# Five score runs for two groups of heads instead of six, with the values' products in the same step, and another rule for the order of the queues

## The chip, the cores and the metric

The kernel runs on one core of a Trainium2 chip. Its engines are named as in the profile: PE (TensorE) multiplies matrices, DVE (VectorE), ACT (ScalarE) and POOL (GpSimd) work on elements, and SP (SyncE) issues most of the DMA transfers. The metric is the device time of one execution in microseconds (us), as the median of several runs.

## The reference

The program is one transformer layer in which attention and a ternary feed-forward network read the same normalized input, and both are added to the input. There are 16 batch rows of 512 tokens, width 512, 16 heads of 32, hidden width 1408. Attention is causal.

```python
def layer(x, w_qkv, b_qkv, w_out, b_out, gate_w, up_w, down_w, gate_s, up_s, down_s):
    xn = layernorm(x)                                     # over 512
    q, k, v = split_heads(xn @ w_qkv.T + b_qkv)           # 16 heads of 32
    scores = q @ k.T / sqrt(32)
    attn = softmax(where(causal, scores, -inf))
    a = merge_heads(attn @ v) @ w_out.T + b_out
    g = (xn @ gate_w.T) * gate_s                          # weights in {-1, 0, 1}
    u = (xn @ up_w.T) * up_s
    f = ((silu(g) * u) @ down_w.T) * down_s
    return x + a + f
```

## The kernel before

**Precision by halves.** Every float32 operand of a product is split into two 16-bit parts, high and low. A product of two split operands is three matmuls (high-high, high-low, low-high), and one with a ternary weight, which is exact in eight bits, is two. So the queries and keys of a group of heads are 12 matmuls of 512 columns each, one hidden chunk of 128 (`ffn_chunk`) is 8 for the gate and 8 for the up projection, a down tile of 128 tokens is 22 and an output tile is 12. All of these go through `mm_group` (line 260) and use the whole 128 x 128 array. The low part comes from a subtraction, on GpSimd for queries and keys (479), hidden values (737) and attention outputs (701), and on VectorE for values (507) and probabilities (621).

**Groups, slots and runs.** Four heads are a group, as they fill the 128 partitions. There are 16 x 4 = 64 groups, and each has a slot of the program. The scores of a group (`soft_run`) are made by blocks of 128 queries: block i sees (i + 1) x 128 keys. Scores of four heads go through four 32-row parts of the array at once (`tile_position`), into four PSUM buffers "s1", one for each head. A group has three runs: block 3 (512 columns), block 2 (384), and blocks 1 and 0 (256 + 128). All three want the same four buffers. For each block and head VectorE takes the row maximum (591), and ScalarE the exponential with its sum (596). Then a block's probabilities of all heads are split into two 16-bit parts (ScalarE 616, VectorE 621) in a buffer "pq", and a DMA transpose that SP issues (630) writes them, transposed, to `pT`, which has one copy. Before, "pq" has two buffers of 4096 elements, and each block is one piece: 2048, 1536, 1024 and 512 elements.

**Values.** `av_step` multiplies `pT` with the values: 72 matmuls on 32-column parts of the array (686). They wait for all four transposes of the group, and the next group's transposes wait for them. `R` is the transposed reciprocal of the exponential sums.

**Fillers.** `fillers` gives each slot full-array work: the queries and keys of the next slot, and the batch row's values, hidden chunks, down tiles and, one row later, output tiles. They use three PSUM buffers "mm".

**The order.** Nothing runs in the order of the program text. Every piece is a `Step` with an engine, an expected duration, a latency and what it reads and writes. `Plan.order` lays all steps out in time by these expected figures: for PE by a key, which spreads fillers and runs over the slot, and at most 20 us ahead of the earliest key that is still open (`AHEAD`); for the other engines by the time a step became ready plus a fixed slack. The steps are then issued in that order, and on the chip each engine keeps it. `begin` asks whether a buffer of a ring is free.

**The start.** The first x, the weights for queries, keys and values and small constants are loaded by SP; gate, up and down weights, which are converted on the way, by nine transfers of GpSimd (`load_gu`, `load_wd`, lines 305 and 314), all after the first queries and keys ("first"). The output weights come in slot 2 (`load_wo`). The residual of a down tile loads x again and adds it and the bias (764 to 768).

## Time and profile before

| | us |
|---|---|
| median of three runs (lowest, highest) | 1895.2 (1893.14, 1897.84) |
| the profiled execution's own time | 1895.28 |
| its span, first to last instruction | 1893.5 |
| PE busy | 1856.3 |
| VectorE busy | 1526.5 |
| ScalarE busy | 1377.2 |
| GpSimd busy | 846.2 |

In the lines shown below, each engine has its busy time, its share of the span and its number of instructions. A line of a timeline gives start, length, engine, line of the kernel, operation, output and inputs, shape and count, and in brackets how long the engine was idle before and what ended that. Matmuls are pipelined: the length of one is longer than the distance from its start to the next. A line of the waits gives who waited for whom, the total, how often, and the longest. A line of a group of instructions ends with busy time, mean length in ns, and idle time before. In a table by stretches, the last three numbers are the granted TensorE clock, the share of the DMA engines that is busy, and GB/s.

### The profile page before, as it was taken

The numbers are of one execution on the slowest core, as the hardware profiler recorded it, in microseconds if no ns is written. First come the engines' busy times: TensorE is split into PE (matmuls) and PEld (weight loads), VectorE is DVE, ScalarE is ACT, GpSimd is POOL, SyncE is SP. The second block draws the span as 40 slices with busy tenths as digits, with TensorE's granted clock in tenths as the row PEclk, the third lists the DMA queues.
The fourth block names the chain that finished last, engine by engine and source line by source line (L and its number), as shares of the span: only waits on it lengthen the run. The fifth ranks groups of instructions, "written<-read, shape, count | busy, mean of one in ns | idle before, by whom it ended". The sixth has DMA issues, their size and how long they took to land. (4 is left out here: it accounts for less than half of the span.)

```text
span 1893.5 us, 40528 instructions
## 1 busy us (share of the span) xinstructions
PE 1856.3 (98%) x15006; PEld 863.7 (46%) x15006; DVE 1526.5 (81%) x3665; ACT 1377.2 (73%) x3179; POOL 846.2 (45%) x649
## 2 busy tenths in 40 slices
PE   7889999999999999999999999999999999999998
PEld 3344444444444444444444444444444444444443
DVE  7888779787887978969788687887979779687684
ACT  6777767778677777777768686786766867777773
POOL 3364444444454444443444444444444444344552
PEclk9999999999999999999999999999999999999999
DMA  8875777777777768767767777587686777676755
GB/s 167 148 160 116 137 148 144 135 143 138 154 143 154 144 129 156 141 145 145 134 136 159 147 152 128 133 157 145 142 148 137 135 162 142 140 144 125 134 112 119
DMA packets 838030, 268.89 MB, mean 142 GB/s; under 512 B 801985, under 2 KB 808513, under 8 KB 837825
## 3 DMA queue, kind: packets, MB, share of 16 engines
q1 hardware_dynamic: 833200, 264.07, 71.4%
q0 software_dynamic: 4624, 2.16, 1.4%
q8 instruction: 119, 1.95, 0.4%
q14 instruction: 87, 0.70, 0.1%
HBM read 55.59 MB, written 16.78 MB: 38 GB/s over the span
## 5 line engine op out<-in xcount | busy, mean ns | idle before, releaser
L596 ACT ACTIVATE p<-s,negm 128x512 f32<-128x512 f32 (+3 forms) x1024 | 531.1, 534 | 267.0 <-DVE negm L591 262.8
L621 DVE SCALAR_TENSOR_TENSOR pq<-p,pq 128x2048 f16<-128x2048 f32 (+3 forms) x256 | 413.8, 1623 | 150.1 <-ACT pq L616 149.2
L591 DVE CUSTOM_DVE_ANT_0 s<-s,mask 128x512 f32<-128x512 f32 (+3 forms) x1024 | 473.1, 518 | 38.5 <-PE s L562 25.3
L737 POOL TENSOR_TENSOR hl<-ft,hh 128x512 f16<-128x512 f32 x176 | 246.1, 1400 | 372.8 <-ACT hh L736 372.6
L616 ACT ACTIVATE pq<-p 128x2048 f16<-128x2048 f32 (+3 forms) x256 | 325.8, 1287 | 8.7 <-DMA pT<-pq 7.3
L260 PE MATMUL u<-xh,wu 128*128 128x512 f16 x704 | 267.4, 380 | 9.4 <-DVE ft L727 6.4
L479 POOL TENSOR_TENSOR qkl<-qkt,qkh 128x512 f16<-128x512 f32 x128 | 160.0, 1250 | 248.0 <-ACT qkh L477 247.6
L260 PE MATMUL g<-xh,wg 128*128 128x512 f16 x704 | 268.0, 381 | 0.3 <-DVE ft L727 0.3
L260 PE MATMUL g<-xl,wg 128*128 128x512 f16 x704 | 267.3, 380 | 0.0
L260 PE MATMUL dn<-wd,hh 128*128 128x512 fp8e4 x704 | 267.3, 380 | 0.0
L260 PE MATMUL u<-xl,wu 128*128 128x512 f16 x704 | 267.3, 380 | 0.0
L260 PE MATMUL dn<-wd,hl 128*128 128x512 fp8e4 x704 | 266.8, 379 | 0.0
L596 ACT ACTIVATION_READ_ACCUMULATOR p<-s,negm 128x1 f32 x1024 | 217.2, 212 | 0.0
L260 PEld LDWEIGHTS <-wu 128*128 128x128 fp8e4 x1408 | 136.4, 98 | 176.8 <-issue 15.1
L260 PEld LDWEIGHTS <-wg 128*128 128x128 fp8e4 x1408 | 134.0, 98 | 164.5 <-issue 7.7
L701 POOL TENSOR_TENSOR ol<-Rs,oh 128x512 f16<-128x512 f32 x64 | 103.3, 1613 | 203.0 <-ACT oh L700 202.8
L736 ACT CAST hh<-ft 128x512 f16<-128x512 f32 x176 | 110.1, 626 | 97.3 <-DVE ft L733 96.6
L727 DVE SCALAR_TENSOR_TENSOR ft<-ft,g 128x512 f32<-128x512 f32 x176 | 119.8, 680 | 51.7 <-ACT ft L723 51.0
L767 POOL TENSOR_TENSOR xr<-xr,bo_b 128x512 f32<-128x512 f32 x64 | 84.4, 1321 | 163.0 <-DMA xr<-in_x 152.3
L723 ACT ACTIVATE ft<-g,gt_c 128x512 f32<-128x512 f32 x176 | 121.8, 692 | 48.0 <-PE g L260 46.4
L260 PEld LDWEIGHTS <-wq_h 128*128 128x128 f16 x1024 | 95.4, 98 | 132.4 <-issue 26.1
L733 DVE SCALAR_TENSOR_TENSOR ft<-u,gu_c,ft 128x512 f32<-128x512 f32 x176 | 132.0, 750 | 23.0 <-PE u L260 9.6
(118 smaller groups left out, 3100.7 us busy)
## 6 DMA issues: line engine op xcount, KB each, us to landing
xc<-in_x SPq DMA_DIRECT2D x64, 256.0 KB, 3.7
xr<-in_x SPq DMA_DIRECT2D x64, 256.0 KB, 3.1
out<-y SPq DMA_DIRECT2D x64, 256.0 KB, 2.6
pT<-pq SPq DMA_TRANSPOSE x256, 5.5
exact<-in_wdT SPq DMA_DIRECT2D x11, 256.0 KB, 2.9
exact<-in_wgT SPq DMA_DIRECT2D x8, 256.0 KB, 2.9
exact<-in_wuT SPq DMA_DIRECT2D x8, 256.0 KB, 3.0
wq<-in_wqkvT SPq DMA_DIRECT2D x2, 768.0 KB, 7.5
```

What stands on the lines that cost most here:

```text
L260: nc.tensor.matmul(ps(), l, r, start=(first + k == 0), stop=(first + k == n - 1))
L479: "POOL", gps(512), lambda: nc.gpsimd.tensor_tensor(l(), t(), h(), ALU.subtract),
L591: nc.vector.tensor_tensor_reduce(sc, sc, mask[:, 512 - n :], -(2.0 ** -7), 3e38, ALU.add, ALU.min, negm()[:, m : m + 1])
L596: nc.scalar.activation(exps(i).rearrange("p (k j) q -> p k j q", j=4)[:, :, j, :], part().rearrange("p (k q) -> p k q", q=P), AF.Exp, bias ...
L616: "ACT", act(4 * n), lambda src=src, half=half: nc.scalar.mul(half(0), src(), 2.0 ** 15),
L621: lambda src=src, half=half: nc.vector.scalar_tensor_tensor(half(1), src(), 2.0 ** 15, half(0), ALU.mult, ALU.subtract),
L701: add("POOL", gps(512), lambda: nc.gpsimd.tensor_tensor(ol(), r(), oh(), ALU.subtract), r=[r, oh], w=[ol])
L723: "ACT", act(512) + 0.1, lambda: nc.scalar.activation(t(), pg(), AF.Tanh, scale=gt_c[:, ic : ic + 1]),
L727: "DVE", dve(512), lambda: nc.vector.scalar_tensor_tensor(t(), t(), 1.0, pg(), ALU.add, ALU.mult),
L733: lambda: nc.vector.scalar_tensor_tensor(t(), pu(), gu_c[:, ic : ic + 1], t(), ALU.mult, ALU.mult),
L736: add("ACT", act(512), lambda: nc.scalar.copy(hh(), t()), r=[t], w=[hh], slack=3)
L737: add("POOL", gps(512), lambda: nc.gpsimd.tensor_tensor(hl(), t(), hh(), ALU.subtract), r=[t, hh], w=[hl])
```

## The change

Two groups, a pair, are handled together by `attention_pair`. Their eight query blocks are packed into five runs of 512 columns: block 3 of the first group; its blocks 2 and 0; block 1 of both; block 3 of the second; its blocks 2 and 0. The values' products of the group before stand in the same step as the second run, behind its scores, and those of the pair's first group with the fourth run (in the last pair, the fifth). The last group's products are a step of their own. Runs keep their order among themselves. Their places in the pair's time are `RUNS`.

The "pq" buffers are four of 2048 elements, and the probabilities of a block are split and transposed in pieces of at most two key blocks, so blocks 3 and 2 have two pieces each and two transposes. The values wait for all six.

`Plan.order` lays the steps out up to six times. After each, `deadlines` works back from the end to the latest time at which each step may start, and the next layout takes steps on DVE, ACT, POOL and SP by that. An engine may be held for up to `WINDOW` for a more urgent step that is about to be ready. PE's steps know the array's shape that they use and leave, a change of shape is given 0.095 us, and of steps that can start at once one of the present shape goes first, where that is not the full array. The expected time of a DMA is other than before.

The fillers are ordered anew: hidden chunks 0 to 3 ahead of values and output tiles, chunks 5 to 10 in the third slot, two down tiles there and two in the fourth. A down tile's first matmuls no longer wait for the last two hidden chunks. At the start only the first 512 columns of gate and up weights load after the first queries and keys; the others wait for the first runs of groups 0, 1 and 2. The output weights load in slot 3, into buffers of the layernorm, and the first batch row's residual is added behind the bias.

```diff
+SWITCH, LANDING = 0.095, 1.4
+WINDOW = 0.5
+RUNS = 0.0, 0.17, 0.30, 0.64, 0.80
+LAST_RUNS = 0.0, 0.14, 0.28, 0.42, 0.56
...
+        best = None
+        for _ in range(times):
+            done = self.layout()
+            if done is None:
+                break
+            end = max(st.end for st in done)
+            if best is None or end < best[0]:
+                best = end, done, [(st.start, st.end) for st in done]
...
+            self.deadlines(done)
...
+    def deadlines(self, done):
+        rings = {}
+        for t in self.tiles():
+            rings.setdefault(t.tag, {})[t.index] = t
+        after = {}
+        for ring in rings.values():
+            for k, t in ring.items():
+                if k >= t.bufs:
+                    first = min(t.users, key=lambda u: u.start)
+                    for u in ring[k - t.bufs].users:
+                        after.setdefault(u, []).append(first)
+        total, at = max(st.end for st in done), {}
+        t = next(st.start for st in done if st.eng == "PE")
+        for st in done:
+            if st.eng == "PE":
+                at[st] = t
+                t += st.dur
+        for st in done[::-1]:
+            late = [x.late - st.lat * (x.eng != st.eng or st.dma) for x in st.next]
+            late += [x.late - st.lat for x in after.get(st, ())]
+            spent = st.end - st.lat - st.start if st.dma else st.dur
+            st.late = min([total] + late) - spent
+            if st.eng == "PE":
+                st.late = min(st.late, at[st])
...
-                    cands = [c for c in cands if c[1].key <= keys[-1][0] + AHEAD]
+                    cands = [
+                        c for c in cands
+                        if c[1].key <= keys[-1][0] + AHEAD or all(b.index is not None for b in c[1].tiles)
+                    ]
...
+                now = [c[1] for c in cands if c[0] <= t0 + 1e-6]
+                if e == "PE":
+                    st = min(now, key=lambda s: (s.mode == "wide" != mode, s.key, s.n))
+                else:
+                    st = min(now, key=lambda s: (s.late, s.n))
+                    if not first:
+                        t1, soon = min(cands, key=lambda c: (c[1].late + (c[0] > t0 + WINDOW) * 1e6, c[1].n))
+                        if t0 + st.dur > max(soon.late, t1) and soon.late < st.late:
+                            t0, st = t1, soon
...
-            if st.eng == "SP":
-                dma = max(dma, t + st.dur) + st.lat
-                st.end = dma + 2.0
+            if st.eng == "PE":
+                if st.mode != mode:
+                    free["PE"] += SWITCH
+                    st.end += SWITCH
+                mode = st.leaves
+            if st.dma:
+                dma = max(dma, t) + st.lat
+                st.end = dma + LANDING
...
-    def mm_group(f, ps, ops, piece=4, first=0, n=None, after=()):
+    def mm_group(f, ps, ops, piece=4, first=0, n=None, after=(), late=0):
...
-            reads = [tok for o in (ops if k0 == 0 else ops[k0:k1]) for tok in o[1]]
+            reads = [tok for o in (ops[: len(ops) - late] if k0 == 0 else ops[k0:k1]) for tok in o[1]]
...
     def load_wo(kc):
-        t = work(f"wo_{kc}", "y", 4)
-        add("SP", 0.5, lambda: nc.sync.dma_start(t(), woT[kc * P : (kc + 1) * P, :]), w=[t], lat=1.3, r=["slot2"])
+        t = work(f"wo_{kc}", "xc", 4)
+        add("SP", 0.5, lambda: nc.sync.dma_start(t(), woT[kc * P : (kc + 1) * P, :]), w=[t], lat=0.85, r=["slot3"])
...
-    def load_gu(c0):
+    def load_gu(c0, when):
...
-                r=["first"], w=[(nm, c0 // 512)], lat=12.0,
...
-    def load_wd(i0, i1):
+                r=when, w=[(nm, c0 // 512)], lat=3.1 * (c1 - c0) / 512,
+            ).dma = True
...
+    def load_wd(i0, i1, when):
...
-            r=["first"], w=[("wd", i0 // 4)], lat=16.0,
-        )
+            r=when, w=[("wd", i0 // 4)], lat=3.1 * (i1 - i0) / 4,
+        ).dma = True
...
-        add("DVE", 1.4, halves, r=["bv", "slot2"], w=[hl])
+        add("DVE", 1.4, halves, r=["bv", "slot3"], w=[hl])
...
-    def soft_run(b, g, blocks):
...
+    def soft_run(parts, values=None):
...
+        qk = lambda s, which: st[s // NG][("qk", s % NG, which)]
+        nm = "_".join(f"{s}{i}" for s, i in parts)
...
-        pq = work("pq_" + nm, "pq", 2, (P, 4096), F16)
+        pqs = [work(f"pq{k}_" + nm, "pq", 4, (P, 2048), F16) for k in range(2)]
         negm = work("negm_" + nm, "negm", 4, (P, 8))
...
+            if values:
+                values[0]()
...
+        more = values[1:] if values else ([], [], 0.0)
         run = add(
-            "PE", 0.21 + 3 * cols / 2400.0, scores, r=[qh, ql, kh, kl],
-            w=[tok for t in pss for tok in both(t)] + ([f"slot{b * NG + g}"] if blocks[0] == 3 else []),
-            lat=0.3,
-        )
-        for u, i in enumerate(blocks):
+            "PE", 0.03 + 3 * cols / 2400.0 + more[2], scores, r=reads + more[0], w=writes + more[1], lat=0.3,
+            after=all_runs[-1:],
+        )
+        all_runs.append(run)
+        run.mode, run.leaves = "rows", "columns" if values else "rows"
+        for s in dict(parts):
+            last_scores[s] = [run]
...
+        turns = []
...
+            for k0 in range(0, i + 1, 2):
+                k1 = min(k0 + 2, i + 1)
+                n, a = 4 * P * (k1 - k0), 4 * (off[u] + k0 * P)
+                pq, a0 = pqs[a // 1024], a % 1024
+                assert a0 + n <= 1024
...
+                add(
+                    "ACT", 0.2 + 0.00085 * n, lambda src=src, half=half: nc.scalar.mul(half(0), src(), 2.0 ** 15),
+                    r=heads, w=[(pq, a0, 0)], slack=2,
+                )
+                add(
+                    "DVE", 0.06 + 0.0012 * n,
+                    lambda src=src, half=half: nc.vector.scalar_tensor_tensor(
...
+                    r=heads + [(pq, a0, 0)], w=[(pq, a0, 1)], slack=2,
+                )
+                to = dst[:, 8 * k0 : 8 * k1, (i % 2) * P : (i % 2 + 1) * P]
+                turns[-1].append(
+                    lambda to=to, flat=flat, pq=pq, a0=a0, i=i, k0=k0, k1=k1: add(
+                        "SP", max(1.2, 1.6 * (k1 - k0) - 1.1), lambda: nc.sync.dma_start_transpose(to, flat()),
+                        r=[(pq, a0, 0), (pq, a0, 1)], w=[("pT", i, k0)], lat=0.19 * 8 * (k1 - k0), slack=-5,
+                    )
+                )
+        return run, turns
...
-        step = add(
-            "PE", 1.86, run, r=[("pT", i) for i in range(4)] + [(t, tb) for t in (vh, vl) for tb in range(NT)],
-            w=[av], lat=0.3,
-        )
...
+        def finish():
...
+        reads = [("pT", i, k) for i in range(4) for k in range(0, i + 1, 2)] + [(t, tb) for t in (vh, vl) for tb in range(NT)]
+        return (run, reads, [av], 1.68 + SWITCH), finish
...
-            piece=4,
+            late=4,
...
-        add(
-            "SP", 0.5, lambda: nc.sync.dma_start(xr(), x[b, tb * P : (tb + 1) * P, :]),
-            r=[y] if b + 1 < NB else [f"slot{NSLOT - 3}"], w=[xr], lat=1.3,
-        )
-        add("POOL", gps(512), lambda: nc.gpsimd.tensor_tensor(xr(), xr(), bo_b, ALU.add), r=[xr, "bo"], w=[xr])
-        add("POOL", gps(512), lambda: nc.gpsimd.tensor_tensor(y(), y(), xr(), ALU.add), r=[xr, y], w=[y], slack=3)
+        def residual():
+            add(
+                "SP", 0.5, lambda: nc.sync.dma_start(xr(), x[b, tb * P : (tb + 1) * P, :]),
+                r=[y] + ["bo"] * (b == 0) if b + 1 < NB else [f"slot{NSLOT - 3}"], w=[xr], lat=0.85,
...
+        if b:
+            residual()
+        else:
+            residuals.append(residual)
...
-    def attention_slot(s):
-        av, runs = None, []
-        if s > 0:
-            av = av_step(*divmod(s - 1, NG))
-        if s < NSLOT:
-            b, g = divmod(s, NG)
-            grp[(b, g)] = dict(den=work(f"den_{b}_{g}", "den", 2, (P, 16)))
-            runs = [(soft_run(b, g, bl), sum((i + 1) * P + 250 for i in bl)) for bl in ((3,), (2,), (1, 0))]
...
-    CUTS = (0, 3, 5, IC, IC)
...
+    def attention_pair(s, f):
+        last = s + 2 == NSLOT
+        values = lambda s: av_step(*divmod(s, NG)) if s >= 0 else (None, lambda: None)
+        turn = lambda fns: [fn() for fn in fns]
+        for k in (s, s + 1):
+            grp[divmod(k, NG)] = dict(den=work(f"den_{k}", "den", 3, (P, 16)))
+        products, finish = values(s - 1)
+        r1, (turn3,) = soft_run([(s, 3)])
+        r2, turns = soft_run([(s, 2), (s, 0)], products)
+        if s:
+            grp[divmod(s - 1, NG)]["step"] = r2
+        finish()
+        turn(turn3 + turns[0] + turns[1])
+        fillers(f, s)
+        r3, (turn0, turn1) = soft_run([(s, 1), (s + 1, 1)])
+        turn(turn0)
+        products, finish = values(s)
+        r4, (turn3,) = soft_run([(s + 1, 3)], None if last else products)
+        if not last:
+            finish()
+            turn(turn1 + turn3)
+        r5, turns = soft_run([(s + 1, 2), (s + 1, 0)], products if last else None)
+        if last:
+            finish()
+            turn(turn1 + turn3)
+        turn(turns[0] + turns[1])
+        fillers(f, s + 1)
+        return r1, r2, r3, r4, r5
...
+    ends, residuals = [], []
...
+    def fillers(f, s):
         b, g = divmod(s, NG)
+        when = [f"slot{s}"]
+        if s < 2:
+            load_gu(512 * (s + 1), when)
+        if s == 2:
+            for i0 in (0, 4, 8):
+                load_wd(i0, min(i0 + 4, IC), when)
+        ffn = lambda *ics: [ffn_chunk(f, b, ic) for ic in ics]
         if s + 1 < NSLOT:
             for which in (0, 1):
                 qk_proj(f, *divmod(s + 1, NG), which)
-        if g == 0 and b == 0:
+        if g == 0:
+            if b:
+                ffn(0, 1, 2, 3)
             for tb in range(NT):
                 v_proj(f, b, tb)
-        late = 2 if b == NB - 1 else NT
-        if b > 0 and g == 1:
-            for tb in range(late):
-                out_tile(f, b - 1, tb)
-        for ic in range(CUTS[g], CUTS[g + 1]):
-            ffn_chunk(f, b, ic)
-        if b > 0 and g == 2:
-            for tb in range(late, NT):
-                out_tile(f, b - 1, tb)
-        if g == 0 and b > 0:
-            for tb in range(NT):
-                v_proj(f, b, tb)
+            if b:
+                for tb in range(NT):
+                    out_tile(f, b - 1, tb)
+            else:
+                ffn(0, 1, 2, 3)
+            ffn(4)
+        if g == 2:
+            ffn(*range(5, IC))
+            for tb in (0, 1):
+                down_tile(f, b, tb)
         if g == 3:
-            for tb in range(NT):
+            for tb in (2, 3):
                 down_tile(f, b, tb)
             if b == NB - 1:
                 for tb in range(NT):
                     ends.append(out_tile(f, b, tb, "s1" if tb < 2 else "mm", NG - 1))
...
-    for c0 in (0, 512, 1024):
-        load_gu(c0)
-    for i0 in (0, 4, 8):
-        load_wd(i0, min(i0 + 4, IC))
+    load_gu(0, ["first"])
...
         b, g = divmod(s, NG)
-        place = attention_slot(s)
-        f = fillers(s)
-        T = f.total + 4.4
...
+        if s % 2 == 0:
+            f = Fill()
+            runs = attention_pair(s, f)
+            T = f.total + 8.4
+            last = s + 2 == NSLOT
+            for run, part in zip(runs, LAST_RUNS if last else RUNS):
+                run.key = start + part * T
+            f.place(start, T)
+            start += T
...
-        if s == 2:
+        if s == 3:
             for kc in range(KC):
                 load_wo(kc)
             f = Fill()
             bias_proj(f)
-            f.place(start + 0.9 * T, 0.1 * T)
+            f.place(start, 2.0)
+            for residual in residuals:
+                residual()
...
         if s == NSLOT - 2:
-            count_good(when, start)
-        start += T
-    attention_slot(NSLOT)(early, 0.0)
+            count_good(when, start - 0.6 * T)
+    (fn, reads, writes, dur), finish = av_step(NB - 1, NG - 1)
+    run = add("PE", dur, fn, r=reads, w=writes, key=start - 0.3 * T, lat=0.3)
+    run.mode = run.leaves = "columns"
+    finish()
     f = Fill()
     for fn in ends:
         fn(f)
...
-    done = plan.order()
+    done = plan.order(6)
```

## The prediction

> **What bounds the kernel now.** I read the page's busy shares first, then stretches of the span, then TensorE's own timeline and waits.
>
> ```profile
> span 1893.5 us, 40528 instructions
> PE 1856.3 (98%) x15006; PEld 863.7 (46%) x15006; DVE 1526.5 (81%) x3665; ACT 1377.2 (73%) x3179; POOL 846.2 (45%) x649
> ```
> ```profile
> core 0: us, PE busy (x) PEld busy (x) DVE busy (x) ACT busy (x) POOL busy (x), PEclk, DMA share, GB/s
> 30.00:74.00 44.00, 39.88 (x291) 17.47 (x292) 36.88 (x88) 31.20 (x70) 13.06 (x12) 0.92 0.94 110
> 200.00:1800.00 1600.00, 1596.10 (x13020) 743.60 (x13018) 1300.12 (x3134) 1185.54 (x2744) 727.15 (x543) 1.00 0.73 142
> 1870.00:1894.00 24.00, 15.34 (x126) 6.93 (x124) 5.88 (x8) 1.98 (x3) 3.90 (x3) 0.85 0.36 91
> ```
>
> In 1600 us of the middle TensorE is idle for 3.9 us in all; VectorE (81%) and ScalarE (74%) have room. So the end is set by what TensorE is given to do, and by idle stretches at both ends, where the granted clock dips too (0.92, 0.85). A full TensorE row can still hide lost time, so I looked at where its matmuls start:
>
> ```profile
> start us, us, engine line op out<-in xcount [idle before <-releaser]
> 614.03 0.38 PE L260 MATMUL g<-xh,wg 128*128 128x512 f16 x1
> 614.25 0.38 PE L260 MATMUL g<-xl,wg 128*128 128x512 f16 x1
> 614.56 0.34 PE L562 MATMUL s<-qkh,qkh 32*128 32x384 f16 x4
> 614.73 0.33 PE L562 MATMUL s<-qkl,qkh 32*128 32x384 f16 x4
> 614.89 0.33 PE L562 MATMUL s<-qkh,qkl 32*128 32x384 f16 x4
> 615.16 0.29 PE L686 MATMUL av<-pT,vh 128*32 128x256 f16 x4
> ```
>
> Full matmuls start 0.216 us apart, score quads of 384 columns 0.163. But the first score starts 0.31 after the last full matmul, and the first values' product 0.27 after the last quad: each change of the array's shape costs about 0.1 more than the work. I did this for the whole timeline: from each block of one shape to the start of the next, less its matmuls at that spacing. There are 492 changes (189 full to scores, 175 back, 47 full to values, 17 scores to values, 62 values to full, 2 values to scores); without the blocks that stalled they cost 0.104 to 0.118 each, 54.6 us in all, **0.111 a change**. The work itself is 1787 us. The rest is stalls:
>
> ```profile
> PE u L260 <- DVE ft L727: 6.4, 8, 1.6
> PE s L562 <- ACT p L596: 3.1, 5, 1.3
> PE u L260 <- ACT qkt L474: 2.9, 1, 2.9
> PE s L562 <- ACT qkh L477: 2.9, 1, 2.9
> PE v L260 <- DVE ft L727: 1.8, 1, 1.8
> PE op L260 <- ACT oh L700: 1.5, 1, 1.5
> ```
>
> By the start-to-start excess, each a little longer than the idle shown: in the first 200 us 3.1 (at 56.6), 1.8 (at 61) and 2.1 in slow-clock matmuls behind these (64 to 67.7); then 1.2 (at 87), 1.4 (103.6), 0.9 (122.6), 4.0 (134), 2.0 (165), together 9.5. In the middle six batches lose 0.98 each: 5.9. At the end 0.5 (1824), 1.8 (1831), 2.5 (1880 to 1883) and 1.5 of slow clock: 6.3.
>
> **The change, part by part.**
>
> *Score runs and values.* Before, a group of heads has three runs of 512, 384 and 384 columns: 192 runs, and 64 blocks of values placed by themselves. After, two groups share five runs of 512: 160, and 63 of the 64 blocks of values stand in the same step as a run. Columns and matmuls stay. Changes after: 160 into a run, 97 from a run to full work, 63 from scores to values, 63 from values to full, 2 around the last values: 385. Saved 107 x 0.111 = **-11.9 us**, on the engine that sets the end, so whole. The Trainium skill (TensorEngine Tiling (Array Packing), Tiling Modes, Key Properties) says that changing the tiling mode drains the engine. Priced as a drain, from rows here, it would be a lone matmul's 0.38 less the 0.216 of one in a stream, 0.164 a change, or -17.5. I take the measured 0.111[...].
>
> *Probability pieces of two key blocks.* Rows before:
>
> ```profile
> L616 ACT ACTIVATE pq<-p 128x2048 f16<-128x2048 f32 x64 | 123.0, 1922 | 0.1
> L616 ACT ACTIVATE pq<-p 128x1024 f16<-128x1024 f32 x64 | 69.3, 1083 | 7.3 <-DMA pT<-pq 7.3
> L621 DVE SCALAR_TENSOR_TENSOR pq<-p,pq 128x2048 f16<-128x2048 f32 x64 | 158.5, 2476 | 116.2 <-ACT pq L616 115.5
> L621 DVE SCALAR_TENSOR_TENSOR pq<-p,pq 128x1024 f16<-128x1024 f32 x64 | 78.8, 1232 | 12.5 <-ACT pq L616 12.5
> ```
>
> ScalarE: 2048 becomes 2 x 1083 (+244 ns), 1536 (1488) becomes 1083 + 654 (+249): 64 x 0.49 = 31.5 us more, 1377 to 1409, 75% of a shorter span. VectorE: -12 and +102 ns, +5.8 us. Both lie under TensorE's work: nothing on the path. On SyncE, 128 more transposes. The Trainium skill's rule speaks against this: many small transfers should be coalesced, and a DMA has a fixed part of about 2.0 us (DMA: Bandwidth & Descriptors, Rules for kernel authors and Anatomy of one DMA; the figure is for the GpSimd path): 128 x 2 = 256 us more of transfer latency, an estimate from that page. The trace says otherwise of this queue: by size (the four transposes of each group in turn) SyncE is held 4.85, 3.96, 1.94 and 1.29 us for 4, 3, 2 and 1 key blocks, landing 6.9, 5.8, 4.4 and 3.4 us after issue. Two of 1.94 replace 4.85, and 1.94 + 1.29 replace 3.96: SyncE is *freed* of 1.7 us a group, 109 of 1183 us. I go by the rows: 0 on the path, and shorter pieces to stand behind on VectorE (1.23 where 2.48 was).
>
> *Loads at the start.* The cause of the first stall is visible:
>
> ```profile
> 37.98 23.71 SPq L630 DMA_TRANSPOSE pT<-pq  x4
> 55.91 1.06 ACT L616 ACTIVATE pq<-p 128x1024 f16<-128x1024 f32 x1 [7.32 <-DMA pT<-pq]
> ```
>
> GpSimd issues nine weight loads between 24.9 and 32.9 us, they land up to 20 us later, and four transposes hold SyncE from 38.0 to 61.7 (one 15.8 us); ScalarE waits for a buffer, and TensorE for ScalarE. After, only two loads are issued there; two wait for group 0, two for group 1, three for group 2. On GpSimd's queue each takes 0.8 us ahead of the subtractions for q, k and hidden values, under TensorE's work; should one be late, the FFN chunk that reads it waits. I take this stall as gone, with its slow clock: 3.1 + 1.8 + 2.1 = **-7.0** (ends -7.0 and 0); late next is then VectorE, for the chunk at 87. The 10.7 us before the first matmul stay.
>
> *Order by deadlines, other moves.* The output weights move from group 2 to 3 (four loads on SyncE, into the layernorm's buffers, ahead of the next x), the first batch's residual waits for the bias; down tiles no longer wait for the last two hidden chunks; v and the output tiles go behind four FFN chunks. Nothing is added; what it does to the stalls I can't count, so half with both ends kept: rest of the start -4.7 (0 to -9.5), middle **-3.0** (0 to -5.9; there VectorE held a range check and eight row maxima ahead of the chunk), end **-3.1** (0 to -6.3, as the last values are keyed 0.3 of a pair ahead of the end).
>
> *New waits.* Values inside a run wait in TensorE's order for all transposes of their group; behind them stand full matmuls, and whoever evacuates them. Also a pair's first run needs q and k from the last filler of the pair before: 0.70 + 0.62 on ScalarE and 1.25 us on GpSimd. Full matmuls of the next pair (allowed 20 us ahead) cover that; uncovered it is some 2.6 us at 16 pairs, 41 us. Between 0 and that, by the nearest row (3.9 us idle in the whole middle): **+5.0**.
>
> Sum: -11.9 - 7.0 - 4.7 - 3.0 - 3.1 + 5.0 = -24.7. Span 1893.5 - 24.7 = 1868.8, plus the 1.8 us that the profiled execution (1895.28) has around its span: **1871 us**. That execution is within 0.1 us of the median of the runs, 1895.2.
>
> **Rivals.** *Only the changes of shape are saved* and the stalls return elsewhere: 1895.2 - 11.9 = 1883. For it: the stalls come from full queues on VectorE and ScalarE, which get no less work. Against: the first stall has a cause that is removed. *Everything goes*: -11.9 - 7.0 - 9.5 - 5.9 - 6.3 = -40.6, 1855. For it: the middle is already nearly without gaps. *Bursts*: runs of 512 let row maxima and exponentials pile up ahead of the chunks' evacuations; at 0.7 us in each of 32 pairs that is 22: 1893. *Slower: values wait for transposes.* Place: each of the 63 fused blocks. Before, transposes landed 2.3 us (least) to 3.7 (median) ahead of their values; the old planner put a four-block transpose at 1.3 + 6.1 + 2.0 = 9.4 us where it takes 6.9, the new one puts one block at 1.5 + 1.4 = 2.9 where it takes 3.4. That margin is spent. Against: the scores ahead of the values give 0.76 us, and from the run to its values there were 20.4 us before, 0.34 x 57 = 19.4 after. It is slower than before by over 0.3% from (24.7 + 5.7)/63 = 0.48 us a block; at 0.7 it gives 1871 + 44 = 1915.
>
> **How the numbers follow.** 0.3% (5.7 us) is about what a measurement of this kernel tells from no change. Chances: forecast 0.57 (its own range 1862 to 1880), changes of shape only 0.20, everything 0.10, bursts 0.05, values' wait 0.08. 1857 to 1889 leaves out half of "everything", the bursts, the wait and a sliver: under 0.2. Under 1889.5 lie 0.57 + 0.19 + 0.10 + 0.01 = 0.87; same 0.05; slower 0.08.
>
> **What would show it.** Right: some 385 changes of shape at 0.11; no transpose that holds SyncE for 15 us near 40 to 60 us; pieces of 1024 at 1.08 and 1.23 us; under 4 us idle in the middle. Wrong: waits of values for pT by the tens, or TensorE under 99% busy between 200 and 1800 us.

## The result

| us | kernel before | changed kernel |
|---|---|---|
| median of the runs (lowest to highest) | 1896.52 of 4 (1893.14 to 1899.87) | 1874.12 of 4 (1873.47 to 1878.95) |
| profiled execution, its span | 1895.28, 1893.5 | 1878.95, 1877.2 |

The ratio is 0.9893, with a 95% interval from 0.9876 to 0.9910: some 20 us faster. The forecast was 1871, the range 1857 to 1889. The profiled execution of the changed kernel is the slowest of its four; the spans of the other three are 1871.6 to 1872.7. Where this matters below, it is said.

First the head of the profile after, its span and the busy shares:

```profile
span 1877.2 us, 41097 instructions
PE 1846.9 (98%) x15006; PEld 874.5 (47%) x15006; DVE 1576.7 (84%) x3793; ACT 1396.5 (74%) x3307; POOL 815.7 (43%) x649
```

TensorE runs the same 15006 matmuls. VectorE has 128 instructions more, as forecast, but 50 us more busy time, not 5.8. The same stretches as before (the last one again ends with the span):

```profile
core 0: us, PE busy (x) PEld busy (x) DVE busy (x) ACT busy (x) POOL busy (x), PEclk, DMA share, GB/s
30.00:74.00 44.00, 42.36 (x322) 19.69 (x321) 39.58 (x107) 33.10 (x81) 12.33 (x11) 1.00 0.89 111
200.00:1800.00 1600.00, 1596.89 (x13082) 757.05 (x13080) 1359.95 (x3273) 1211.87 (x2882) 710.67 (x548) 1.00 0.76 144
1850.00:1878.00 28.00, 17.97 (x138) 7.98 (x136) 8.17 (x13) 4.77 (x14) 6.86 (x5) 0.85 0.58 120
```

In 30 to 74 us TensorE starts 322 matmuls where it started 291, and the clock no longer dips there. In the middle it is as full as before (1596.89 of 1600 us, before 1596.10) and yet starts 62 matmuls more: the busy share does not show the gain, the count of matmuls hints at it. A step that holds a run and the values, on TensorE's timeline (start, duration, engine, line, operation, tiles, shape, count):

```profile
587.09 0.38 PE L338 MATMUL dn<-wd,hl 128*128 128x512 fp8e4 x1
587.40 0.39 PE L644 MATMUL s<-qkh,qkh 32*128 32x512 f16 x4
587.63 0.38 PE L644 MATMUL s<-qkl,qkh 32*128 32x512 f16 x4
587.84 0.38 PE L644 MATMUL s<-qkh,qkl 32*128 32x512 f16 x4
588.16 0.29 PE L783 MATMUL av<-pT,vh 128*32 128x256 f16 x4
588.28 0.28 PE L783 MATMUL av<-pT,vl 128*32 128x256 f16 x4
...
589.76 0.23 PE L783 MATMUL av<-pT,vh 128*32 128x128 f16 x4
589.92 0.39 PE L338 MATMUL dn<-wd,hh 128*128 128x512 fp8e4 x1
```

Three changes of shape: 0.31, 0.32 and 0.16 us from start to start, where streams of these sizes have 0.216, 0.216 and 0.054. So each costs about 0.1, and no stall lies between the scores and their values. Counted so over the whole timeline, in the way of the prediction but with the slow first matmuls taken in on both sides:

| us of TensorE's time | before | after |
|---|---|---|
| changes of shape | 492, 54.6 | 385, 43.0 |
| stalls and slow clock to 200 us | 22.7 | 17.5 |
| stalls 200 to 1800 us | 5.7 | 7.3 |
| stalls behind 1800 us | 4.1 | 2.7 |
| behind the last matmul | 6.0 | 6.7 |

The differences add up to -15.9; the spans differ by 16.3. The medians differ by 22: the three runs that were not profiled are about 5 us shorter, so a usual run should hold about 22.5 us of stalls instead of 27.5, if its changes cost the same (an estimate: 27.5 less 1877.2 - 1872.3, the span that belongs to the median). That is the low end: a second profile of the same program, with a span of 1872.9 (the preference alone, below), holds 25.4. What TensorE waits for (us in total, times, longest):

```profile
PE lnT L513 <- DVE xc L483: 10.7, 1, 10.7
PE u L338 <- DVE ft L826: 6.5, 9, 3.4
PE s L644 <- ACT p L688: 1.6, 3, 0.9
PE op L338 <- ACT oh L798: 1.5, 1, 1.5
```

No line with `av` and `pT` is among them. The longest wait behind the first matmul is a single one of 3.4 us, and it has the same chain as the stall that was forecast to go. GpSimd, SyncE, ScalarE, VectorE and TensorE on the timeline after:

```profile
75.77 1.55 POOL L395 DMA_DIRECT2D wd<-in_wdT  x2
...
80.56 0.78 POOL L395 DMA_DIRECT2D wd<-in_wdT  x1
...
77.06 18.58 SPq L728 DMA_TRANSPOSE pT<-pq  x3
...
91.67 1.06 ACT L715 ACTIVATE pq<-p 128x1024 f16<-128x1024 f32 x1 [3.81 <-DMA pT<-pq]
...
92.76 1.22 DVE L720 SCALAR_TENSOR_TENSOR pq<-p,pq 128x1024 f16<-128x1024 f32 x1 [3.72 <-ACT pq L715]
93.90 0.68 DVE L826 SCALAR_TENSOR_TENSOR ft<-ft,g 128x512 f32<-128x512 f32 x1
...
94.63 0.39 PE L338 MATMUL u<-xh,wu 128*128 128x512 f16 x1 [3.40 <-DVE ft L826]
94.85 0.60 PE L338 MATMUL u<-xl,wu 128*128 128x512 f16 x1
```

The loads that now wait for group 2 are in flight from 76 us; three transposes hold SyncE for 18.6 us; ScalarE waits for a probability buffer, VectorE for ScalarE, TensorE for VectorE. Behind the stall matmuls take 0.60 where they take 0.38: the clock granted from 94.6 to 99.0 us is 0.61. The stall has moved from 56 to 91 us. With the slow clock this block loses 6.1 us here; in four other profiles with the same order of instructions (below) it loses 2.1 to 3.2.

### The profile page after: what moved, and what is told of

It reads as the page before. It is cut to its first block, busy times and chain, and to the rows that moved or that the text cites. A ratio compares the mean times of both kernels' runs of the same rounds, so it can differ in the third digit from the quotient of the medians.

```text
span 1877.2 us, 41097 instructions
## 1 busy us (share of the span) xinstructions
PE 1846.9 (98%) x15006; PEld 874.5 (47%) x15006; DVE 1576.7 (84%) x3793; ACT 1396.5 (74%) x3307; POOL 815.7 (43%) x649
## 5 line engine op out<-in xcount | busy, mean ns | idle before, releaser
L720 DVE SCALAR_TENSOR_TENSOR pq<-p,pq 128x1024 f16<-128x1024 f32 (+1 forms) x384 | 473.5, 1258 | 29.2 <-ACT pq L715 27.0
L836 POOL TENSOR_TENSOR hl<-ft,hh 128x512 f16<-128x512 f32 x176 | 224.3, 1278 | 281.8 <-ACT hh L835 281.2
L715 ACT ACTIVATE pq<-p 128x1024 f16<-128x1024 f32 (+1 forms) x384 | 339.0, 920 | 9.6 <-DMA pT<-pq 7.6
L688 ACT ACTIVATION_READ_ACCUMULATOR p<-s,negm 128x1 f32 x1024 | 210.8, 206 | 0.0
L799 POOL TENSOR_TENSOR ol<-Rs,oh 128x512 f16<-128x512 f32 x64 | 82.6, 1290 | 208.6 <-ACT oh L798 205.1
L769 POOL TENSOR_TENSOR Rs<-R 128x512 f32<-128x512 f16 x64 | 83.5, 1304 | 167.7 <-DMA R<-rb 167.6
L555 ACT ACTIVATE qkt<-qk,bqk_c 128x512 f32<-128x512 f32 x128 | 88.3, 691 | 85.0 <-PE qk L338 73.2
```

What stands on the lines that cost most here:

```text
L555: "ACT", act(512) + 0.1, lambda: nc.scalar.activation(t(), ps(), AF.Identity, bias=bias, scale=sc),
L688: nc.scalar.activation(exps(u).rearrange("p (k j) q -> p k j q", j=4)[:, :, j, :], part().rearrange("p (k q) -> p k q", q=P), AF.Exp, bias ...
L715: "ACT", 0.2 + 0.00085 * n, lambda src=src, half=half: nc.scalar.mul(half(0), src(), 2.0 ** 15),
L720: lambda src=src, half=half: nc.vector.scalar_tensor_tensor(half(1), src(), 2.0 ** 15, half(0), ALU.mult, ALU.subtract),
L769: lambda: nc.gpsimd.tensor_tensor(r(), R()[:, 0:4, :].rearrange("p i q -> p (i q)"), R()[:, 4:8, :].rearrange("p i q -> p (i q)"), ALU.add),
L836: add("POOL", gps(512), lambda: nc.gpsimd.tensor_tensor(hl(), t(), hh(), ALU.subtract), r=[t, hh], w=[hl])
```

## The experiments

The theory under test was the prediction's: some 12 us come from 107 changes of shape at 0.111 us, some 7 from the weight loads that no longer stand in front of the transposes, and the rest from an order with fewer stalls. The rival: the planner's deadlines carry the stalls, and the placing of loads and pieces nothing. Ratios are to the kernel before, run on the same chip, with 95% intervals. All are changes to the changed kernel unless it is said that they start from the one before.

**Is a change of shape worth 0.11 us?** Two kernels with the instructions in the order of the changed kernel, as their traces show. Each adds one small full matmul to the 63 fused steps, whose result is overwritten: in one between scores and values, where it makes one change more (scores to full, full to values), in the other ahead of the scores, where it makes none.

```diff
             for u, (s, i) in enumerate(parts):
 ...
             if values:
+                full()      # e11_full_between; in e12_full_ahead ahead of the scores
                 values[0]()
```

> The changed kernel in its own order, with one full-array matmul of 128 columns (0.056 us, its result is overwritten) between the scores and the values of each of the 63 fused steps. This makes 63 more changes of shape, 448 in all, and nothing else moves. My theory (a change costs 0.111 us on the path): 63 x (0.056 + 0.111) = 10.5 us more than the changed kernel, and 7.0 us more than the same matmul ahead of the scores. Rival (the stalls behind take up what the changes cost, as values apart may show): at most 2 us more than the same matmul ahead of the scores.

> The changed kernel in its own order, with the same 63 full-array matmuls of 128 columns ahead of the scores of the fused steps, where TensorE is in the full shape anyway: no change of shape more. Both theories: 63 x 0.056 = 3.5 us more than the changed kernel, 1876 to 1879 us; it is the other end of the comparison.

Measured: between 1884.90 (6 runs; ratio 0.9944, 0.9931 to 0.9957), ahead 1878.17 (5 runs; 0.9911, 0.9895 to 0.9926). The matmul alone costs 4.0 us over the changed kernel, the change of shape 6.73 more: 6.73 / 63 = 0.107 us each. TensorE's timeline with the matmul between:

```profile
587.99 0.39 PE L649 MATMUL s<-qkh,qkl 32*128 32x512 f16 x4
588.31 0.23 PE L638 MATMUL av<-wq_h 128*128 128x128 f16 x1
588.47 0.29 PE L789 MATMUL av<-pT,vh 128*32 128x256 f16 x4
```

The 0.32 from scores to values has become 0.32 + 0.16. Of these 0.16, 0.054 are the matmul's own columns and 0.106 the second change. At a fixed order the stalls do not absorb it: a change of shape is paid in the run time at the price read from the timeline.

**Values in steps of their own.** Two kernels: without the planner's preference for the present shape, and with it.

```diff
-        r2, turns = soft_run([(s, 2), (s, 0)], products)
+        r2, turns = soft_run([(s, 2), (s, 0)])
         if s:
-            grp[divmod(s - 1, NG)]["step"] = r2
+            grp[divmod(s - 1, NG)]["step"] = r2.values = apart(products)
 ...
+                    run.values.key = run.key + 0.03 * T
 ...
-                    st = min(now, key=lambda s: (s.mode == "wide" != mode, s.key, s.n))
+                    st = min(now, key=lambda s: (s.key, s.n))     # e1_values_apart alone
```

> The changed kernel, with the values' products a step of their own, keyed 0.03 of a pair (1.7 us) behind their run, and no preference for staying in a shape. My theory (changes of the array's shape cost 0.111 us each and lie on the path): 385 + 63 = 448 changes, 63 x 0.111 = 7.0 us more than the changed kernel, 1881 us. Rival (the new order of the queues makes the gain, the count of changes only goes with it): 1874 us, give or take 2.

> The changed kernel with the preference kept, and values a step of their own keyed 0.03 of a pair behind their run, which they may follow directly where they are ready. Theory one (the preference makes the stalls): changes of shape 385 to 420, stalls about 25, 1873 to 1878 us. Theory two (the fused step makes the stalls): the same changes with stalls of about 13, 1864 to 1869 us.

Measured: without preference 1872.89 (0.9877, 0.9861 to 0.9893), with it 1875.14 (0.9887, 0.9871 to 0.9904); the changed kernel has 1874.12. Without preference there are 448 changes, 63 more, which at 0.11 are the 6.9 us expected. But this order has 13.1 us of stalls, 1.9 of them in the middle, where the two profiles of the changed kernel's program have 27.5 and 25.4. With the preference there are about 393 changes and 21.0 us of stalls (12.4 in the middle). So fusing does save its changes of shape, but the kernel without it is as fast: in these three orders the stalls give or take as much again. One part of it is visible. In these two kernels no transpose issued beside the weight loads holds SyncE for more than 7.6 us (5.3 with the preference), where one holds it for 12.7 in the changed kernel. Why the loads hold the transposes less here, and why the first order has so few stalls in the middle, was not found.

**The preference alone.**

```diff
-                    st = min(now, key=lambda s: (s.mode == "wide" != mode, s.key, s.n))
+                    st = min(now, key=lambda s: (s.key, s.n))
```

> The changed kernel with only the preference for staying in a shape taken out of the order of TensorE; values stay in the step of their run, so the changes of shape stay at 385. In the profile of values apart, which also lacked this preference, there were 448 changes but stalls of only 13.1 us where the changed kernel has 27.5. Theory one (the preference makes the stalls, by putting a run ahead of full matmuls as soon as it can start): stalls about 13, so 1866 us. Theory two (the fused step makes them, as a run with values must wait for all transposes before it may be placed): stalls about 25, 1874 us.

Measured: 1874.37 (0.9875, 0.9859 to 0.9892), 385 changes, 25.4 us of stalls. With scores and values fused the preference decides nothing: in the two traces the instructions of all five engines stand in the same order. So this is a second measurement of the changed kernel's program, and it shows what the stall is like in another run: the block that lost 6.1 us there (the 3.4 us wait and the slow clock) loses 3.2 here. Neither theory of this run and of the own steps with preference holds in both. That the preference makes the stalls is refuted here; that the fused step makes them would have had 13 us of stalls and at most 1869 us there, and 21.0 and 1875.14 were measured.

**The weight loads.** First the kernel *before* with only the loads spread as in the changed kernel:

```diff
-    for c0 in (0, 512, 1024):
-        load_gu(c0)
-    for i0 in (0, 4, 8):
-        load_wd(i0, min(i0 + 4, IC))
+    load_gu(0, ["first"])
 ...
+        when = [f"slot{s}"]
+        if s < 2:
+            load_gu(512 * (s + 1), when)
+        if s == 2:
+            for i0 in (0, 4, 8):
+                load_wd(i0, min(i0 + 4, IC), when)
```

> The kernel before with only the weight loads spread as in the change: the second and third piece of gate and up at groups 0 and 1, down weights at group 2. As predicted (the stall at 56 to 68 us goes): 7.0 us less than before, 1889 us. Rival, from the profile after (the stall only moves to where the down weights load): 1894 to 1897 us, with a transpose that holds SyncE for over 10 us behind the down weights' loads.

Measured: 1893.01 (12 runs) against 1896.81 (15), ratio 0.9984, 0.9975 to 0.9992: -3.8 us (by the ratio -3.0), not -7. A stretch of this kernel's span (columns as in the table of stretches above), and a line of SyncE's timeline:

```profile
30.00:74.00 44.00, 44.00 (x336) 20.24 (x334) 41.62 (x109) 37.01 (x90) 13.81 (x13) 1.00 0.85 120
```
```profile
81.21 10.76 SPq L630 DMA_TRANSPOSE pT<-pq  x1
```

The stall at 56 us is gone entirely (44.00 of 44.00, clock 1.00). But the loads issued at 75 us hold a transpose for 10.8 us, and TensorE stalls 3.6 us at 75 and 2.2 at 97, where the kernel before lost 1.2 (at 87) and 1.4 (at 103.6). (A stall of 2.6 us at 123 has its like there at 134.) About half of the gain is given back. The time lies between the two that were forecast, nearer to the rival's.

Then the changed kernel with all nine loads at once, at the old place and at a much earlier one:

```diff
-    load_gu(0, ["first"])
+    for c0 in (0, 512, 1024):
+        load_gu(c0, ["first"])      # e7_loads_early: [("wqh", 1, 0)]
+    for i0 in (0, 4, 8):
+        load_wd(i0, min(i0 + 4, IC), ["first"])      # the same
```

> The changed kernel with all nine weight loads behind the first queries and keys, as before. As predicted: 7.0 us more than the changed kernel, 1881 us. Rival (the stall only moved): it goes from around 91 us back to around 50 us, and the time stays within 2 us of 1874.

> The changed kernel with all nine weight loads already behind the first pieces of the query and key weights (about 9 us), so that most have landed before the first transposes at 34 us. My theory (weight loads of GpSimd's queue in flight hold the transposes, and those hold ScalarE and TensorE): stalls of the first 200 us fall from 17.5 us in the profile to about 9, 1868 us. Rival (the transposes wait for something else, or the loads delay the query, key and value weights by as much): 1874 us or more.

Measured: at the old place 1872.44 (0.9874, 0.9857 to 0.9890), early 1875.36 (0.9887, 0.9870 to 0.9903). SyncE with the loads at the old place, and TensorE's waits with the early ones:

```profile
31.27 26.86 SPq L728 DMA_TRANSPOSE pT<-pq  x5
```
```profile
PE lnT L513 <- DVE xc L483: 14.9, 1, 14.9
PE qk L338 <- ACT qkt L555: 4.3, 2, 3.0
```

At the old place five transposes hold SyncE for 26.9 us, one of them for 12.4, as before the change; but TensorE loses only 2.0 us at 30, 1.0 at 43 and 5.2 at 133, and the time is not longer than the changed kernel's. The spreading is not where the gain comes from. With early loads no transpose is held longer than 4.4 us, so the hold does go away with the loads; but the 1868 us that this was to give did not come. Early loads run against the q and k weights instead: the first matmul starts at 14.9 instead of 10.7 us.

**Pieces of whole blocks,** as before the change, in two large probability buffers:

```diff
-        pqs = [work(f"pq{k}_" + nm, "pq", 4, (P, 2048), F16) for k in range(2)]
+        pq = work("pq_" + nm, "pq", 2, (P, 4096), F16)
 ...
-            for k0 in range(0, i + 1, 2):
-                k1 = min(k0 + 2, i + 1)
+            for k0, k1 in ((0, i + 1),):
 ...
```

> The changed kernel with two probability buffers of 4096 and one piece and one transpose a block, as before. My theory (the pieces lie beside TensorE's work): 1874 us, give or take 2, with 31 us less on ScalarE. Rival one (the rule to coalesce transfers counts here): 128 fewer transposes make it faster, 1868 us. Rival two (a piece of 2.5 us on VectorE stands ahead of the chunks' evacuations): some ten more waits of 0.8 us in the middle, 1882 us.

Measured: 1875.31 (0.9884, 0.9868 to 0.9901), stalls 25.8 us. Halving the pieces moves nothing that can be measured, in either direction, and 128 transposes more cost nothing.

**The order without deadlines.** `order` lays the steps out six times, each time with the deadlines worked out from the last layout, and takes the shortest. With one layout no deadline is known, no engine is held for a more urgent step, and queues go by when a step could start plus its slack:

```diff
-    done = plan.order(6)
+    done = plan.order(1)
```

> The changed kernel with one layout only, so without deadlines: the queues of VectorE, ScalarE, GpSimd and SyncE go by ready time plus slack, as before. My theory: still 385 changes; the stalls of the kernel before come back at most, 5 us: 1874 to 1880 us. Rival (deadlines make the gain): 1884 us or more.

Measured: 1993.12 (ratio 1.0503, 1.0482 to 1.0524), with the same 385 changes of shape. TensorE's waits and the middle of the span (columns as above):

```profile
PE av L783 <- DMA pT<-pq: 41.1, 27, 3.4
PE s L644 <- ACT p L688: 22.0, 26, 2.7
PE u L338 <- DVE ft L826: 21.6, 23, 4.9
```
```profile
200.00:1800.00 1600.00, 1526.17 (x12135) 716.82 (x12133) 1280.20 (x3069) 1112.19 (x2669) 671.82 (x506) 0.98 0.70 134
```

This is the prediction's slower rival, seen on the chip: values wait for transposes, 27 times, and the full matmuls behind them wait too. Stalls are 147 us, 119 more than in the changed kernel; the values' waits, 41.1, are the largest line of them, not the whole. The theory's number, 1880 at most, is missed by over 110 us; the rival, that the deadlines matter, holds by far more than the few us that were to tell the two apart. (The kernel before has no deadlines either, and no such waits. What in the changed kernel makes it need them, the fused steps, the packing or the other expected times, no run shows.)

**The new planner alone,** in the kernel before: its layout, deadlines, expected durations and preference, and the output weights in the layernorm's buffers; six runs a pair, whole pieces and loads at once stay.

```diff
-                st = min(
-                    (c[1] for c in cands if c[0] <= t0 + 1e-6),
-                    key=lambda s: (s.key, s.n) if e == "PE" else (s.at + s.slack, s.n),
-                )
+                now = [c[1] for c in cands if c[0] <= t0 + 1e-6]
+                if e == "PE":
+                    st = min(now, key=lambda s: (s.mode == "wide" != mode, s.key, s.n))
+                else:
+                    st = min(now, key=lambda s: (s.late, s.n))
 ...
-    done = plan.order()
+    done = plan.order(6)
```

> The kernel before (six runs, values apart, whole pieces, all weight loads at once) with the new planner alone: deadlines, six layouts, the new expected times, the shape's preference; output weights in the layernorm's buffers so that an order exists. My theory: about 480 changes, stalls fewer by up to 8 us: 1888 to 1896 us. Rival (the planner makes the gain): 1874 to 1880 us.

Measured: 1883.83 (0.9934, 0.9917 to 0.9951), between the two theories' numbers. It has about 470 changes of shape (22 fewer, 2.4 us) and 22.0 us of stalls where the kernel before has 32.5. The remaining 9.7 us to the changed kernel (7.8 by the ratios) are about what 85 changes of shape cost at 0.11: 9.4. Which part of the planner brings the fewer stalls was not taken apart here.

**The third run later.** In the middle several third runs of a pair start late, as ScalarE's last exponentials free the score buffers one by one: some 3.6 us. So their key and those behind were moved:

```diff
-RUNS = 0.0, 0.17, 0.30, 0.64, 0.80
+RUNS = 0.0, 0.17, 0.34, 0.66, 0.82
```

> The changed kernel with the third to fifth run keyed later, at 0.34, 0.66 and 0.82 of the pair instead of 0.30, 0.64 and 0.80. Nine of the third runs wait for ScalarE, 0.3 to 1.0 us each, as the second run's last exponentials free the four score buffers one by one. My theory: these 3.8 us in the middle go, 1870 us. Rival (every edit of the keys gives another order with other waits of the same size, and values come nearer to their transposes): 1874 us, give or take 3.

Measured: 1877.29 (0.9891, 0.9873 to 0.9909), stalls 27.6 us. The keys moved nothing: all instructions of all engines stand in the order of the changed kernel. So neither the theory nor the rival was tested, and why these runs start late stays argued, from the buffers that they wait for. What this run does give is a third measurement of one program.

No kernel here is clearly faster than the changed one: the shortest medians, 1872.44 and 1872.89, have ratios of 0.9874 and 0.9877, and their intervals overlap that of the changed kernel's 0.9893. The same program, measured three times, has medians of 1874.12, 1874.37 and 1877.29, so that differences of 3 us between these kernels say nothing. Not run were the packing into five runs without the rest, the new order of the fillers, and fused steps under the old planner.

## Why the prediction was right, point by point

**Changes of shape, -11.9: right in count and price.** 385 were forecast and 385 are there; by kind they cost 0.104 to 0.118, and at a fixed order 0.107. That they count whole, "on the engine that sets the end", holds at a fixed order only: with values apart 63 of the 107 changes come back, and the time does not. The price worked out as a drain from the lone matmul, 0.164, which was weighed beside the Trainium skill's rule (TensorEngine Tiling (Array Packing), Tiling Modes, Key Properties), would have been half as much again. The page gives no price; the spacing on the timeline does.

**Loads at the start, -7.0: the step that failed.** "I take this stall as gone" was right for its place and wrong for TensorE's sum. The loads were only moved; at 76 us they meet transposes too, with the same chain down to the slow clock, for 2.1 to 6.1 us. Alone the spreading brings 3.0 to 3.8 us, and without it the changed kernel loses nothing. "Late next is then VectorE, for the chunk at 87" did name the place of the new stall, but gave it no price.

**Rest of the start -4.7, middle -3.0, end -3.1: the sum about right, its parts not.** The profile has -5.2 for the whole start, loads included (forecast -11.7), +1.6 in the middle (forecast -3.0 and, for new waits, +5.0) and -1.4 at the end. All stalls together were forecast to fall by 12.8; in the profiled run they fall by 5.0, and in a usual run by 7 (the second profile) to 10 (the estimate above). The order's moves had -10.8 of this, half of the stalls there were, because they couldn't be counted. The planner alone, with loads and runs as before, brings 10.5, in other places (it gains nothing in the middle), and the loads bring nothing. So the new planner carries the stalls' part, and that half was its size is luck.

**New waits, +5.0: the size near, the place another.** No values wait for transposes and no run for q and k in numbers that matter. Some 3.6 us are third runs behind ScalarE's exponentials.

**Pieces, 0 on the path: right.** Going back to whole blocks costs and brings nothing. The rule on small transfers (the Trainium skill, DMA: Bandwidth & Descriptors, Rules for kernel authors and Anatomy of one DMA) would have had 256 us of latency there, an estimate; none of it reaches the end. (Its row puts mostly overhead under 64 KB; the smallest piece here has 256 KB.) But two sizes beside the path were off. The pieces after, by shape:

```profile
L715 ACT ACTIVATE pq<-p 128x1024 f16<-128x1024 f32 x256 | 268.2, 1062 | 9.3 <-DMA pT<-pq 7.3
L715 ACT ACTIVATE pq<-p 128x512 f16<-128x512 f32 x128 | 78.1, 635 | 0.2 <-DMA pT<-pq 0.2
L720 DVE SCALAR_TENSOR_TENSOR pq<-p,pq 128x1024 f16<-128x1024 f32 x256 | 357.6, 1405 | 28.1 <-ACT pq L715 25.9 <-DMA xc<-in_x 1.6
L720 DVE SCALAR_TENSOR_TENSOR pq<-p,pq 128x512 f16<-128x512 f32 x128 | 120.5, 964 | 1.1 <-ACT pq L715 1.0
```

ScalarE's are as priced (1083 and 654 forecast). VectorE's take 1405 and 964 instead of 1232 and 826, in sum 478.1 us where the pieces before took 415.4: more than the whole 50 us by which the engine's busy time grew. The forecast took means of rows, and these hold different shares of waiting for GpSimd (last section): without it, pieces of 4, 3, 2 and 1 key blocks take 2.28, 1.76, 1.22 and 0.68 us, those of 2 and 1 in both kernels, so that smaller pieces cost 0.29 us a group, 18 us in all. Another 49 are more of such waits (84.1 less 34.8). SyncE was to be freed of 109 us in transposes of values; these held it for 807 us before and hold it for 783 now, 24 less. The rows of before promised 1.72 us a transpose (10.34 for the six of a group); measured are 2.04 on average.

**The slower rival, values wait, 0.08: not in the changed kernel, but real.** Its break-even was 0.48 us a block. With deadlines the wait is nothing; without them it is the largest line of TensorE's waits, and the kernel is 5% slower than before. The changed layout and the deadlines belong together, and the prediction had counted them as separate items. The rival *changes of shape only*, 1883, is what the stalls' part makes too long; *everything goes*, 1855, is refuted by the stalls that stay.

The forecast is 3.1 us below the median. It stands on one term that was measured to be right at a fixed order (changes of shape) and on a sum over the stalls that came out about right while its parts moved: too much for the loads, and for the order a half that nothing had been counted for. In that sum there is luck.

## What to carry to other kernels

Where an engine looks full, read the spacing of its starts: a change of the array's shape cost 0.1 us here, was paid in full at a fixed order, and hid inside a busy share of 99.8%. A stall whose cause is a transfer is not gone when the transfer is moved: price what it meets at its new place. And a denser layout, with more work behind each wait, may be right only together with an order that knows when each step is due; test the two apart before crediting either. And where a planner stands between an edit and the chip, compare the order of instructions in the two traces first: two edits here changed nothing, and their times are the noise of one program.

## What was not expected of the hardware

A VectorE piece that starts while a tensor operation of GpSimd is under way lasts longer by the rest of that operation. Two pieces of one shape, and GpSimd beside the second:

```profile
92.76 1.22 DVE L720 SCALAR_TENSOR_TENSOR pq<-p,pq 128x1024 f16<-128x1024 f32 x1 [3.72 <-ACT pq L715]
...
96.11 1.16 POOL L560 TENSOR_TENSOR qkl<-qkt,qkh 128x512 f16<-128x512 f32 x1
...
96.25 2.10 DVE L720 SCALAR_TENSOR_TENSOR pq<-p,pq 128x1024 f16<-128x1024 f32 x1 [0.80 <-ACT pq L715]
```

When the second starts, GpSimd has 1.02 us left; the piece takes 0.88 more than the first. Of the 384 pieces after, 119 start so, and they add up to 84.1 us of such extra time. In the 112 of them where GpSimd had more than 0.2 us left, the extra is what was left less 0.13 to 0.14 us, each time. Of the 265 others, many with a GpSimd operation that starts later beside them, none takes more than 1.23 us (128x1024) or 0.69 (128x512). Before, 71 of 256 pieces start so, with 34.8 us. No run took GpSimd's work away, but the measure fits each piece.

In several orders one transpose that is issued while GpSimd's weight loads are in flight holds SyncE far longer than the rest: 15.8 us before, 12.7 after, 10.8 with the loads spread in the kernel before and 12.4 with all at once in the changed one. The place follows the loads, and with early loads there is none. But not each transpose beside a load is held so: others in these four traces are held for 1.2 to 6.5 us, and away from the loads the longest has 5.6. What singles one out stays open.

The layouts with medians from 1872.44 to 1875.36 hold between 13.1 and 27.5 us of stalls in their profiled executions, in other places from order to order; one program alone spans 25.4 to 27.6 in three profiles. Why the one with values apart stalls least stays open.
